# Self attention on one Trainium2 core: the values projected in tiles of 128 tokens instead of one tile per batch

## The chip, the cores and the metric

The kernel runs on one core of one Trainium2 chip. Its time is the device time of one execution in microseconds (us). Times are given for three runs of the kernel, and one further execution was recorded by the hardware profiler. A core has a matrix engine (PE, whose weight loads are listed apart as PEld), a vector engine (DVE), an activation engine (ACT), a general engine (POOL) and a sync engine (SP) that issues most of the DMAs. Each takes its instructions in order. Matrix results land in PSUM, which is divided into banks; everything else that is on the chip lies in SBUF, in 128 partitions.

## The reference

The kernel computes one decoder layer in float32 with three blocks, each followed by a residual sum and a normalisation: causal self attention (16 heads of 32), cross attention to a context of 361 tokens (16 heads of 128, four key and value heads), and a mixture of 8 experts of which each token uses 2. There are 16 batches of 100 tokens, with 512 features. The part that matters here:

```python
def _L0_attn_ref(x, w_q, w_k, w_v, w_o):            # x: 16 x 100 x 512
    q = (x @ w_q.T).reshape(b, s, NH, HD).transpose(0, 2, 1, 3)
    k = (x @ w_k.T).reshape(b, s, NH, HD).transpose(0, 2, 1, 3)
    v = (x @ w_v.T).reshape(b, s, NH, HD).transpose(0, 2, 1, 3)
    score = einsum('bhqd,bhkd->bhqk', q, k) * scale, masked causally
    o = einsum('bhqk,bhkd->bhqd', softmax(score), v)
    return o.transpose(0, 2, 1, 3).reshape(b, s, H) @ w_o.T

x = _layernorm(x + _L0_attn_ref(x, ...))
x = _layernorm(x + _L0_xattn_ref(x, ctx_2048, ...))
x = _layernorm(x + _L0_ffn_ref(x, ...))
```

The projection of the values, `x @ w_v.T`, does not know of batches: row t of the result depends on row t of x alone. The product of the softmax with v does: it needs the 100 value rows of one batch, from partition 0 on.

## The kernel before

Products in float32 precision are made from three faster ones. `split` (lines 137 to 140) writes a rounded high part of a tile on one engine and the remainder as a low part on another. `mm3` (lines 145 to 147) multiplies high by high, high by low and low by high, and `mmk` does that for the four blocks of 128 features (`KC`). So one projected tile takes 12 matmuls.

**Self attention** takes the batches in four groups (`NG`) of four (`GB`), 400 tokens each (`GT`). The input x comes transposed, features on the partitions, so x of a group is 128 x 4 x 400. A group has four chunks of 128 features, that is of four heads, and the pair of group and chunk is a unit (g, c); there are 16 units, numbered u = 4g + c. In a unit:

- `self_q` and `self_k` project 128 features of all 400 tokens, 12 matmuls each with 400 columns.
- `self_scores` makes 16 small matmuls of scores, and `self_softmax` spreads the softmax of each head j over DVE (mask and minimum, L358 and L361; sums, L367), POOL (L363 and L380) and ACT (L366 and L370).
- `self_turn` transposes the probabilities of head j on PE (L393), and ACT copies them to SBUF (L395).
- `self_attend` multiplies with the values (L405), and ACT copies the result (L415), which SP stores to DRAM as `o1d` (L416).
- `self_v(g, r)` projects the values of batch r of group g for all 512 features: 12 matmuls with the x of the batch's 100 tokens as the stationary operand and 512 columns of weights streaming. Its result has 100 rows. ACT copies it to the tile `V[g, r]` (L309). All four tiles of a group must be there when `self_attend(g, 0)` begins. PSUM results of `self_v` use the tag "mm", for group 0 the tag "t"; each tag has two banks.

The order of work inside a unit comes from a table `extra`, filled by `at(u, j, f, ...)`: f runs in unit u just before head j is turned. While unit u is turned and attended, the scores of unit u + 1 are already made, the projections of unit u + 2 are placed at j = 0 and 2, the next group's x is loaded in the unit c = 0 and split in c = 0 and 1, and its values are projected in c = 2 and 3, two tiles in each. Group 0's values are projected at the start. A scheduler then sorts the instructions by a modelled timeline, so what is written next to each other may be interleaved with other work.

**The way into the next block.** During the last units the outputs of self attention are loaded back by tiles of 128 tokens (`b_fetch`, lines 435 and 438), split (`b_split`), multiplied with w_o (`b_out`, 12 matmuls `pa`, then the residual sum and the norm on DVE), and turned (`b_xT`, L460). `b_open` closes the pool `a_x` of the inputs x, whose memory the loaded tiles `ol` and `xr` reuse. All of these have hand-set places in the units, with i = 4u + j as the position. After unit 15 the queries of the cross attention (`b_q`) follow.

Pools rotate a fixed number of buffers under one tag. The tag "f" of the pool `xp`, with two buffers, serves some of the weight chunks of 128 x 512 that are loaded and split in the first units (`chunk`), and tag "v" has eight buffers, two groups' worth.

Of the kernel before, what the change touches and what calls it, by code (L numbers as in the profile page):

```python
# [9 lines left out]
FP = mybir.dt.float32  # L10
# [7 lines left out]
B, S, D = 16, 100, 512  # L18
T = B * S
KC = D // 128  # L20
# [8 lines left out]
GB = 4  # L29
NG = B // GB  # L30
GT = GB * S
# [31 lines left out]
def tile_decoder_layer(  # L63
# [28 lines left out]
    nc = tc.nc  # L92
# [3 lines left out]
    def pool(stack, name, bufs=1, **k):  # L96
        return stack.enter_context(
            tc.tile_pool(name=name, bufs=bufs, reuse_waits="tile", **k)
        )
# [6 lines left out]
    def bank(tag, shape, name):  # L106
        return ps[-1].tile(shape, FP, name=name, tag=tag)
# [12 lines left out]
    def in_turn(ins, prev):  # L120

        if prev is not None:
            tc.add_manual_dep(
                ins.ins,
                prev.ins.name,
                mybir.DependencyInfo(
                    mybir.DependencyClass.NoSync, mybir.DependencyReason.DATA
                ),
                reason="in_turn",
            )  # L130
        return ins

    def split(dst, src, high=None, low=None):

        high, low = high or nc.scalar, low or nc.vector
        if high is nc.scalar:
            ins = nc.scalar.copy(dst.h, src)  # L137
        else:
            ins = high.tensor_copy(dst.h, src)  # L139
        low.tensor_tensor(dst.l, src, dst.h.bitcast(FP), ALU.subtract)  # L140
        return ins

    def mm3(out, a, b, start, stop):

        nc.tensor.matmul(out, a.h, b.h, start=start, stop=False)  # L145
        nc.tensor.matmul(out, a.h, b.l, start=False, stop=False)  # L146
        nc.tensor.matmul(out, a.l, b.h, start=False, stop=stop)  # L147

    def mmk(out, a, b, n=KC):
        for k in range(n):  # L150
            mm3(out, a(k), b(k), k == 0, k == n - 1)
# [44 lines left out]
    def slot_of(s):  # L196
        return Pair(WH[:, s], WL[:, s])
# [8 lines left out]
    units = {}  # L206
# [15 lines left out]
    a_l, a_r = ExitStack(), ExitStack()  # L222
    xp = pool(a_r, "a_x", 1, side="right")
    w1 = pool(a_l, "a_1", 1)
    w2 = pool(a_l, "a_2", 2)
    w3 = pool(a_l, "a_3", 8)
    ps.append(pool(a_l, "ps_a", 2, space=PSUM))
    ps_s = pool(a_l, "ps_s", 1, space=PSUM)

    xg, V, Q, K, O, P = {}, {}, {}, {}, {}, {}  # L230
# [26 lines left out]
    def chunk(n, c, queue=None):  # L257

        cc = slice(c * 128, (c + 1) * 128)
        chunks.append(n)  # L260
        p, bufs = (xp, 2) if len(chunks) % 5 > 2 else (stage, 3)
        f = p.tile([128, KC, 128], FP, name=f"f_{n}_{c}", tag="f", bufs=bufs)
        if n == "v":
            f = f.rearrange("p k n -> p (k n)")
            part, dst = src[n][:, c], units["wv_s"][:, c]
        else:
            part, dst = src[n][:, :, cc], units[f"w{n}_s"][:, :, cc]
        (queue or nc.sync).dma_start(f, part)
        return dst, f
# [24 lines left out]
    for k in range(KC):  # L294
        split(*chunk("v", k, nc.scalar), low=nc.vector if k == 2 else nc.gpsimd)

    def split_chunk(c):
        split(*chunk("q", c), nc.scalar, nc.gpsimd)
        split(*chunk("k", c), nc.scalar, nc.gpsimd)

    def self_v(g, r):
        pv = bank("mm" if g else "t", [S, D], f"pv_{g}_{r}")
        mmk(
            pv,
            lambda k: xg[g][:, k, r * S : (r + 1) * S],
            lambda k: units["wv_s"][:, k, :],
        )
        V[g, r] = w1.tile([S, D], FP, name=f"v_{g}_{r}", tag="v", bufs=8)
        nc.scalar.copy(V[g, r], pv)  # L309

    def self_q(g, c):
        cc = slice(c * 128, (c + 1) * 128)
        pq = bank("mm", [128, GT], f"pq_{g}_{c}")
        mmk(pq, lambda k: units["wq_s"][:, k, cc], lambda k: xg[g][:, k, :])

        Q[g, c] = w2.tile([128, GT], FP, name=f"qT_{g}_{c}", tag="qT")
        nc.scalar.activation(Q[g, c], pq, AF.Copy, scale=-1.0 / math.sqrt(HD1))
# [79 lines left out]
    def self_attend(g, c):  # L397

        av = bank("t", [128, GB, S], f"av_{g}_{c}")
        prev = None  # L400

        for r in range(GB):
            for j in (3, 0, 1, 2):
                h = c * 128 + 32 * j
                ins = nc.tensor.matmul(  # L405
                    av[32 * j : 32 * j + 32, r, :],
                    V[g, r][:, h : h + 32],
                    PT[g, c, j][:, r, :],
                    start=True,
                    stop=True,  # L410
                    tile_position=(0, 32 * j),
                )
                prev = in_turn(ins, prev)
        o = w2.tile([128, GT], FP, name=f"o_{g}_{c}", tag="o")
        nc.scalar.copy(o, av.rearrange("p r s -> p (r s)"))  # L415
        nc.sync.dma_start(o1d[g][:, c], o)  # L416
# [51 lines left out]
    def at(u, j, f, *a):  # L468
        extra.setdefault((u, j), []).append(lambda: f(*a))
# [24 lines left out]
    for u, (g, c) in enumerate(heads4):  # L494
        if u + 2 < NU:
            if u < 2:
                at(u, 0, split_chunk, u + 2)
            at(u, 0, self_k, *heads4[u + 2])
            at(u, 2, self_q, *heads4[u + 2])
        if g + 1 < NG:  # L500
            if c == 0:
                at(u, 1, fetch_x, g + 1)
                for k in range(2):
                    at(u, 3, split_x, g + 1, k)
            if c == 1:
                for k in range(2):
                    at(u, 1, split_x, g + 1, 2 + k)
            if c > 1:
                for r in range(2):
                    at(u, 1 + 2 * r, self_v, g + 1, 2 * (c - 2) + r)  # L510

    rows = [("wo_s", 3, kp(woT), k) for k in range(KC)]
    rows += [("wq_0", 4, Wqg[0], k) for k in range(KC)]
# [8 lines left out]
    for k in range(KC):  # L522
        i = 4 * NU - 8 + k
# [2 lines left out]
        at(i // 4, i % 4, behind, split_row, "wq_3", k)  # L526

    AHEAD = 5
    at(10, 0, b_open)
    for t, i in enumerate((44, 48, 52, 54, 58)):  # L530
        at(i // 4, i % 4, b_fetch, t)
        i += 2 if t == AHEAD - 1 else 4
        at(i // 4, i % 4, behind, b_split, t)
    for t, i in enumerate((51, 55, 59, 61, 62)):
        at(i // 4, i % 4, b_out, t)
    for t, i in enumerate((57, 60, 63)):
        at(i // 4, i % 4, b_xT, t)
# [2 lines left out]
    self_k(0, 0)  # L540
    self_scores(*heads4[0])
    self_v(0, 0)
    split_chunk(1)
    for r in range(1, GB):
        self_v(0, r)
    self_q(0, 1)
    self_k(0, 1)
    for u, unit in enumerate(heads4):
        if u + 1 < NU:
            self_scores(*heads4[u + 1])  # L550
        for j in range(4):
            for f in extra.get((u, j), []):
                f()
            self_turn(*unit, j)
        self_attend(*unit)
# [8 lines left out]
    w1 = pool(b_l, "b_1", 1)  # L564
# [113 lines left out]
    w1 = pool(c_l, "c_1", 1, side="right")  # L678
# [183 lines left out]
    for i, (b, g) in enumerate(order):  # L862
# [34 lines left out]
        if i % 3 == 2 and 8 <= i < 8 + 3 * NKV * KC:  # L897
            w, k = divmod((i - 8) // 3, KC)
# [12 lines left out]
    w1 = pool(d_l, "d_1", 1, side="right")  # L911
# [408 lines left out]
    for i in range(HEAD * NKV, len(parts)):  # L1320
        t, g = parts[i]
# [453 lines left out]
```

## Time and profile before

| | |
|---|---|
| median of 3 runs | 1432.21 us (1428.25 to 1441.84) |
| the profiled execution | 1437.28 us, its span 1435.6 us |
| mean granted clock of PE | 0.973 |
| self attention | about 0 to 207 us |
| cross-attention queries, keys and values, attention, output | about 207 to 1100 us |
| experts and the last norm | about 1100 to 1436 us |
| PE MATMUL pv of L145, L146 and L147 (self attention) | 64 each, median 392 to 394 ns |
| ACT COPY v<-pv of L309 | 16, median 585 ns |

The span runs from the first to the last instruction of the program; 1.7 us of the profiled execution's time lie outside it. Busy times are unions of the instructions' times on an engine. Matmuls overlap one another in the pipeline, so the time that one takes from a full engine is the distance between starts, not its own duration. In the views below, "L145" is line 145 of the kernel, and `pv<-WH` means that the instruction writes tile pv and reads tile WH.

### The profile page before, as it was taken

How to read it: one execution, taken by the hardware profiler on the slowest of the kernel's cores; microseconds unless marked ns; L12 is line 12 of the kernel's file. 1: busy time of each engine (PE TensorE's matmuls, PEld its weight loads, DVE VectorE, ACT ScalarE, POOL GpSimd, SP SyncE). 2: the span in 40 equal slices, each digit the busy share in tenths (PEclk: the TensorE clock that was granted, in tenths of full speed). 3: DMA queues.
4: the chain of work that ended last, by engine and by line, in shares of the span. 5: the costliest groups of instructions: out<-in, count | busy, mean ns of one | idle time of the engine just before them, and what ended most of it. 6: DMA issues, size and time to landing. Idle time of an engine off the chain costs nothing. (4 is left out here: it accounts for less than half of the span.)

```text
span 1435.6 us, 25188 instructions
## 1 busy us (share of the span) xinstructions
PE 1342.1 (93%) x7952; PEld 1107.7 (77%) x7952; DVE 954.1 (66%) x2978; ACT 746.8 (52%) x1872; POOL 731.1 (51%) x854
## 2 busy tenths in 40 slices
PE   8999989999999999999999999999999897988884
PEld 6888878888778888888888888878887674666663
DVE  5766667775567777777777667767555559653698
ACT  4666643444436666566666566656553232332353
POOL 6877653443335555555555455545444445343542
PEclk9999999999999999999999999999999998899898
DMA  5221254555442232323233222223536554666674
GB/s 157 71 92 53 70 161 111 135 92 110 98 103 62 62 74 51 74 63 75 69 75 70 74 68 69 50 65 76 131 81 200 179 165 129 210 227 214 209 239 139
DMA packets 197873, 159.79 MB, mean 111 GB/s; under 512 B 133322, under 2 KB 152878, under 8 KB 197742
## 3 DMA queue, kind: packets, MB, share of 16 engines
q1 hardware_dynamic: 187904, 137.83, 36.2%
q0 software_dynamic: 4576, 14.95, 3.4%
q10 hardware_dynamic: 5262, 5.41, 1.3%
q8 instruction: 65, 1.06, 0.3%
q14 instruction: 66, 0.54, 0.1%
HBM read 107.16 MB, written 50.99 MB: 110 GB/s over the span
## 5 line engine op out<-in xcount | busy, mean ns | idle before, releaser
L759 POOL TENSOR_SCALAR p<-p,sums 100x361 f32<-100x361 f32 x256 | 146.4, 576 | 100.3 <-DVE sums L758 89.3
L746 DVE CUSTOM_DVE_ANT_0 p<-s,nmask 100x361 f32<-100x361 f32 x256 | 132.9, 527 | 64.7 <-PE s L147 56.2
L757 ACT ACTIVATE p<-p,nm 100x361 f32<-100x361 f32 x256 | 153.2, 602 | 39.8 <-DVE nm L746 36.5
L140 DVE TENSOR_TENSOR pT_l<-ptp,pT_h 128x400 fp32r<-128x400 f32 (+1 forms) x192 | 107.4, 567 | 59.3 <-ACT pT_h L137 58.8
L145 PE MATMUL pq<-WH 128*128 128x512 f32 (+2 forms) x272 | 106.5, 392 | 6.2 <-DVE WH L139 5.8
L767 PE MATMUL ptp<-ident,p 100*128 100x100 f32 (+1 forms) x768 | 107.6, 252 | 0.0
L140 POOL TENSOR_TENSOR cT_l<-cf,cT_h 128x512 fp32r<-128x512 f32 (+1 forms) x48 | 54.4, 1134 | 104.2 <-ACT cT_h L137 102.3
L137 ACT CAST pT_h<-ptp 128x400 fp32r<-128x400 f32 (+1 forms) x192 | 91.3, 487 | 30.2 <-PE ptp L767 29.7
L767 PEld LDWEIGHTS ptp<-ident,p 100*128 100x128 f32 (+1 forms) x768 | 95.6, 152 | 13.5 <-POOL p L759 2.3
L146 PE MATMUL pq<-WL,WH 128*128 128x512 f32 (+2 forms) x272 | 104.1, 383 | 0.0
L147 PE MATMUL pq<-WH,WL 128*128 128x512 f32 (+2 forms) x272 | 103.8, 382 | 0.0
L147 PE MATMUL acc<-WH,ot_l 128*128 128x512 f32 (+1 forms) x208 | 87.3, 421 | 8.7 <-DVE ot_l L140 6.9
L145 PE MATMUL acc<-WH,ot_h 128*128 128x512 f32 (+1 forms) x208 | 87.2, 419 | 5.5 <-ACT ot_h L137 5.5
L145 PE MATMUL s<-kT_h,WH 128*100 128x362 f32 x256 | 88.5, 356 | 2.4 <-ACT kT_h L137 2.4
L145 PE MATMUL av<-pT_h,WH 128*128 128x400 f32 (+1 forms) x192 | 77.1, 401 | 11.6 <-ACT pT_h L137 11.1
L146 PE MATMUL acc<-WL,ot_h 128*128 128x512 f32 (+1 forms) x208 | 85.1, 409 | 0.0
L147 PE MATMUL s<-kT_h,WL 128*100 128x362 f32 x256 | 84.5, 330 | 0.0
L146 PE MATMUL s<-kT_l,WH 128*100 128x362 f32 x256 | 83.9, 328 | 0.0
L614 POOL TENSOR_TENSOR qs<-qs,r_q 128x512 f32<-128x512 f32 (+1 forms) x52 | 54.0, 1068 | 58.0 <-DVE r_q L169 47.5
L140 POOL TENSOR_TENSOR WL<-qf,WH 128x400 fp32r<-128x400 f32 x64 | 67.3, 1051 | 31.0 <-ACT WH L137 27.7
L145 PE MATMUL pv<-WH,cT_h 128*128 128x512 f32 (+1 forms) x192 | 80.0, 417 | 1.3 <-DVE WL L140 1.3
L145 PE MATMUL pk<-WH,cT_h 128*128 128x512 f32 (+1 forms) x192 | 77.7, 405 | 0.2
(330 smaller groups left out, 4030.0 us busy)
## 6 DMA issues: line engine op xcount, KB each, us to landing
qf<-qd SPq DMA_DIRECT2D x64, 200.0 KB
of<-od SPq DMA_DIRECT2D x48, 256.0 KB
cf<-in_ctxT SPq DMA_DIRECT2D x16, 722.0 KB
eb<-in_expert_b SPq DMA_DIRECT2D x32, 256.0 KB
ysd<-xs SPq DMA_DIRECT2D x32, 256.0 KB
f_e<-in_expert_w SPq DMA_DIRECT2D x30, 256.0 KB
f_wq<-in_Wq SPq DMA_DIRECT2D x16, 256.0 KB
f_wo<-in_Wo SPq DMA_DIRECT2D x16, 256.0 KB
```

Of the source, the lines that this page charges most:

```text
L137: ins = nc.scalar.copy(dst.h, src)
L140: low.tensor_tensor(dst.l, src, dst.h.bitcast(FP), ALU.subtract)
L145: nc.tensor.matmul(out, a.h, b.h, start=start, stop=False)
L146: nc.tensor.matmul(out, a.h, b.l, start=False, stop=False)
L147: nc.tensor.matmul(out, a.l, b.h, start=False, stop=stop)
L614: nc.gpsimd.tensor_tensor(qr[:, hs, :], qr[:, hs, :], rs[:n, hs].unsqueeze(2).to_broadcast([n, GR, HD2]), ALU.mult,)
L746: nc.vector.tensor_tensor_reduce(out=p, in0=sc[:, :SE], in1=nmask, scale=1.0, scalar=BIG, op0=ALU.add, op1=ALU.min, accum_out=nm,)
L757: nc.scalar.activation(p, p, AF.Exp, bias=nm, scale=-1.0, accum_out=sh)
L759: nc.gpsimd.tensor_scalar(p, p, sh, 1.0, ALU.mult, ALU.mult)
L767: nc.tensor.transpose(pt[:n, h, :], probs[h][:, c0 : c0 + n], ident[:S, :S])
```

## The change

A group's 400 tokens make three tiles of 128 and a rest of 16 tokens. The rests of the four groups, 64 tokens, are gathered into one more tile. So the values take 4 x 3 + 1 = 13 tiles of 12 matmuls.

- At the start, four DMAs from ACT's queue load the last 16 tokens of each group's x into `xl_f`, which DVE and POOL split into a part of weight slot 5. `self_v_last` projects these 64 tokens once and keeps them in `v_last`.
- `self_v(g, t)` now projects 128 tokens. Tile 0 is copied by ACT to `V[g, 0]`, which has 128 rows; tiles 1 and 2 are copied to `vt`, with the buffers of tag "f" in `xp`. DMAs from SP, from SBUF to SBUF, then put the rows at their batches: 28 rows of tile 0 to batch 1; 72 and 56 rows of tile 1 to batches 1 and 2; 44 and 84 rows of tile 2 to batches 2 and 3; 16 rows of `v_last` to batch 3. That is six DMAs a group.
- `self_attend` reads the first 100 rows of each V.
- Values of the next group: two tiles in the unit c = 2, one in c = 3. At the start, `self_v_last` stands between tile 0 and tiles 1 and 2.
- Since `xp` is needed longer, `b_open` moves from unit 10 to unit 12, and the first places of `b_fetch`, `b_split` and `b_out` move later.

```diff
+    w4 = pool(a_l, "a_4", 1)
...
+    REST_V = GT % 128
+    xl_f = xp.tile([128, KC, 4 * REST_V], FP, name="xl_f", tag="f", bufs=2)
+    for g in range(NG):
+        nc.scalar.dma_start(
+            xl_f[:, :, g * REST_V : (g + 1) * REST_V], xT[g][:, :, GT - REST_V :]
+        )
+    xl = slot_of(5)[:, :, : 4 * REST_V]
+    split(xl, xl_f, nc.vector, nc.gpsimd)
+    v_last = w4.tile([4 * REST_V, D], FP, name="v_last")
...
-    def self_v(g, r):
-        pv = bank("mm" if g else "t", [S, D], f"pv_{g}_{r}")
+    def self_v_last():
+        pv = bank("mm", [4 * REST_V, D], "pv_last")
+        mmk(pv, lambda k: xl[:, k, :], lambda k: units["wv_s"][:, k, :])
+        nc.scalar.copy(v_last, pv)
+
+    def self_v(g, t):
+        pv = bank("mm" if g else "t", [128, D], f"pv_{g}_{t}")
         mmk(
             pv,
-            lambda k: xg[g][:, k, r * S : (r + 1) * S],
+            lambda k: xg[g][:, k, t * 128 : (t + 1) * 128],
             lambda k: units["wv_s"][:, k, :],
         )
-        V[g, r] = w1.tile([S, D], FP, name=f"v_{g}_{r}", tag="v", bufs=8)
-        nc.scalar.copy(V[g, r], pv)
+        for r in range(GB) if t == 0 else ():
+            V[g, r] = w1.tile([128, D], FP, name=f"v_{g}_{r}", tag="v", bufs=8)
+        vt = V[g, 0] if t == 0 else xp.tile([128, D], FP, name=f"vt_{g}_{t}", tag="f", bufs=2)
+        nc.scalar.copy(vt, pv)
+        a = S if t == 0 else t * 128
+        while a < (t + 1) * 128:
+            r, o = divmod(a, S)
+            m = min(S - o, (t + 1) * 128 - a)
+            nc.sync.dma_start(V[g, r][o : o + m], vt[a - t * 128 : a - t * 128 + m])
+            a += m
+        if t == 2:
+            nc.sync.dma_start(
+                V[g, GB - 1][S - REST_V : S], v_last[g * REST_V : (g + 1) * REST_V]
+            )
...
-                    V[g, r][:, h : h + 32],
+                    V[g, r][:S, h : h + 32],
...
-            if c > 1:
-                for r in range(2):
-                    at(u, 1 + 2 * r, self_v, g + 1, 2 * (c - 2) + r)
+            if c == 2:
+                at(u, 1, self_v, g + 1, 0)
+                at(u, 3, self_v, g + 1, 1)
+            if c == 3:
+                at(u, 1, self_v, g + 1, 2)
...
-    at(10, 0, b_open)
-    for t, i in enumerate((44, 48, 52, 54, 58)):
+    at(12, 0, b_open)
+    for t, i in enumerate((48, 50, 52, 54, 58)):
         at(i // 4, i % 4, b_fetch, t)
-        i += 2 if t == AHEAD - 1 else 4
+        i += 2 if t in (0, AHEAD - 1) else 4
         at(i // 4, i % 4, behind, b_split, t)
-    for t, i in enumerate((51, 55, 59, 61, 62)):
+    for t, i in enumerate((53, 56, 59, 61, 62)):
         at(i // 4, i % 4, b_out, t)
...
-    for r in range(1, GB):
-        self_v(0, r)
+    self_v_last()
+    for t in range(1, 3):
+        self_v(0, t)
```

## The prediction

> **What bounds the kernel now.** I read the page first: its busy table, then its slices.
>
> ```profile
> span 1435.6 us, 25188 instructions
> PE 1342.1 (93%) x7952; PEld 1107.7 (77%) x7952; DVE 954.1 (66%) x2978; ACT 746.8 (52%) x1872; POOL 731.1 (51%) x854
> PE   8999989999999999999999999999999897988884
> PEclk9999999999999999999999999999999998899898
> ```
>
> The matrix engine is busy 93% of the span and full in nearly every slice, so a matmul removed from a full stretch should shorten the run by its pace. The change lives in self attention, the first 207 us, so next come busy times by stretch (columns: length, then busy us of PE, PEld, DVE, ACT, POOL, then granted clock, DMA share, GB/s).
>
> ```profile
> 45.00:90.00 45.00, 44.85 (x473) 37.68 (x472) 29.55 (x71) 28.02 (x85) 32.52 (x37) 1.00 0.24 78
> 90.00:135.00 45.00, 44.84 (x471) 37.69 (x469) 28.46 (x65) 28.56 (x83) 35.41 (x40) 1.00 0.25 85
> 135.00:165.00 30.00, 30.00 (x325) 24.18 (x324) 17.91 (x44) 19.85 (x58) 22.65 (x25) 1.00 0.16 50
> 165.00:207.00 42.00, 37.76 (x368) 31.48 (x367) 33.08 (x78) 25.09 (x68) 30.95 (x32) 0.92 0.41 121
> ```
>
> From 45 to 165 PE never rests; the others have a quarter to a third of their time free. The last 42 us, which I call the tail, are different: PE loses 4.2 us and the clock falls. The waits of PE, first in 20 to 180 us, then in 180 to 215:
>
> ```profile
> PE pv L145 <- ACT v L309: 1.3, 2, 1.1
> PE pt L393 <- POOL p L380: 0.2, 1, 0.2
> ...
> PE pt L393 <- ACT pT L395: 2.8, 2, 2.4
> PE av L405 <- ACT pT L395: 1.4, 2, 0.8
> ```
>
> Last the timeline of PE. It gives the pace of a value matmul (start to start, which a busy time of 0.39 us hides, since matmuls overlap), and the tail's gap with the slow stretch after it:
>
> ```profile
> 151.94 0.45 PE L145 MATMUL pv<-WH 128*100 128x512 f32 x1
> ...
> 154.54 0.39 PE L147 MATMUL pv<-WH,WL 128*100 128x512 f32 x1
> 154.77 0.51 PE L393 MATMUL pt<-ident,p 100*100 100x100 f32 x4
> ...
> 191.13 0.55 PE L393 MATMUL pt<-ident,p 100*100 100x100 f32 x4 [2.38 <-ACT pT L395]
> ...
> 196.76 0.63 PE L145 MATMUL pa<-WH,olp_h 128*128 128x512 f32 x1
> 197.19 0.63 PE L146 MATMUL pa<-WL,olp_h 128*128 128x512 f32 x1
> ...
> 199.05 0.40 PE L145 MATMUL pa<-WH,olp_h 128*128 128x512 f32 x1
> 199.29 0.40 PE L146 MATMUL pa<-WL,olp_h 128*128 128x512 f32 x1
> ```
>
> One value tile of 12 matmuls takes 154.77 - 151.94 = 2.83 us of PE. After the gap of 2.38 us a matmul takes 0.43 us until 198.8, then 0.24 again.
>
> **What the Trainium skill says.** "TensorE: Matmul & The Clock Gate", Step-by-step: a matmul costs what it streams, one moving column a cycle; how many output rows it has does not enter. The trace agrees: pv with 100 rows runs at 0.231 us, pa with 128 rows at 0.228. So a 128-token tile costs PE what a 100-token tile costs. Same page, Part 1: the clock halves when PE has been idle in a window of some 3.4 us. Here a shorter gap, 2.38 us, was followed by nearly half the pace, so the measurement decides. "DMA: Bandwidth & Descriptors", Anatomy of one DMA: about 2.0 us fixed plus bytes over 436 GB/s. The trace has no copy inside SBUF; its nearest kind is the 200 KB store of o, whose landing mark comes 1.9 us after issue when alone and up to 5 us among bulk loads. The same page, "Why a DMA increments its semaphore by 16 and not by 1": the engines used are the largest number up to 16 that divides the rows, so 44 rows use 11 and 28, 56 and 84 use 14: no copy falls on a single engine. No run here shows that yet.
>
> **The change, part by part.**
>
> *Matmuls removed.* 16 tiles become 13: 36 of 192 value matmuls go (PE's built program shrinks from 7200 to 7164 rows). The first group still runs four tiles (0, 1, 2 and the shared rest of 64 rows), so the start gains nothing; each later group loses one tile, in its predecessor's last unit. 3 x 2.83 = 8.5 us, all where PE is full.
>
> *Weight loads.* 128 columns instead of 100: 188 ns for 164 (the rows of pa and pv). Both are under the pace of 231, so hidden; uncovered they would be 156 x 24 ns = 3.7 us.
>
> *Evictions.* ACT makes 13 copies instead of 16 at 585 ns: 1.8 us less, of no worth on an engine with a third free.
>
> *V copies.* 24 new DMAs on SP, six a group. About 0.33 us of issue each, 8 us of an SP that mostly waits (83 us for o alone). 2.5 MB more traffic: 1200 packets of 2 KB at 84 ns over 16 engines, 6 us of a queue busy 20%. Latency I bound between 1.9 us (lone store) and 5.5 (among loads) and take 2.2. Who waits: the first attend matmul of a group, and behind it PE's whole queue. From the end of tile 2 to that attend PE has two projections (2.2 us each), two score blocks (0.9 each), an attend and four or more transposes: about 10 us. The path is eviction 0.6, two issues 0.7, landing 2.2, with ACT's queue ahead perhaps 1 to 2: some 5.5. Hidden with 4 us to spare; at 5.5 us of latency just hidden. Cost 0, at most 1 us a group.
>
> *The shared rest at the start.* Four loads on ACT's queue, 2048 packets of 64 B at 11 ns (as the 64 B packets of ol took): 1.4 us on each DMA engine. ACT issues them while it waited anyway (0.53 and 0.91 us idle before f_q and qT), and the f_q cast moves behind qT. The cast of 128x256 is half of 0.43 us on DVE and the low part half of 1.3 us on POOL, between 16 and 22 us, where DVE had 3.0 us idle. The load of f_q for chunk 2 now waits for a slot of vt, so for two V copies: it moves from 11.8 us to about 24.5, lands near 27.5, and its cast stands in ACT's queue ahead of the first big exponentials (27.3 before). POOL's low part then ends near 30.5; PE asks for it at 34.15. Against that, two matmuls of the rest fill part of the 1.1 us wait for a PSUM bank. Bounds -0.5 and +1.5; I take 0.
>
> *The tail.* b_open moves from unit 10 to 12, since the pool of x now lives until the last vt is copied; the loads of ol and xr move past the V copies on SP, the splits of ol and two of the five output projections (12 matmuls pa each) later. In the built order 36 pa matmuls followed the last scores; now 46 to 48 do, and DVE takes the last softmax before the norm of tile 0. The PE work from the first transpose of unit 12 to the last attend is equal: pq and pk 3 x 2.2, five pa blocks 5 x 2.76, scores 1.8, attends 3.4, transposes about 7.5, sum some 33 to 35 us. Before, it ran from 165.2 to 206.9, 41.7 us: 4.2 us of waits and about 2.8 us from the slow clock. Walking the new order with the durations of before, the last scores end near 15 us after that first transpose, their softmax near 25 (POOL, with two ol splits ahead of it, is the latest), and PE asks for it at 30. The transposes of unit 14 then wait on ACT and DVE for 1 to 2 us in pieces instead of 2.4 in one, so the slow clock should not come. Bounds 0 and 7; I take 5.
>
> *Later stages.* The order is the same up to the experts; there some loads, stores and transposes move by a few places. PE has 63 us idle in the last 436, so it can go either way; I take 0, bounds -4 and +4.
>
> *Sum.* 1437.3 (the profiled execution's own time; 1.7 of it lies outside the span) - 8.5 - 5 = 1423.8. The median of the runs is 5.1 below that execution, so 1432.2 - 13.5 = 1418.7, say 1419.
>
> **Rivals.**
>
> (B) Only the matmuls count: the tail is bound by the chain score, softmax, ACT copy, which starts 8.5 us sooner but stalls as before. For: it was ACT, not PE, that ended the tail's waits. Against: more pa work now covers it. 1432 - 8.5 = 1424.
>
> (C) The gain is lost: softmax of the short units falls behind once the long unit has 2.83 us less cover. For: the first transposes of units 1 and 6 had under 1.5 us between POOL's end and their start. Against: those units hold as many matmuls before as after; where a tile goes, the spare was 7 us or more. 1429 to 1433.
>
> (D) Slower: V copies land late. Place: the first attend of each group, PE's queue behind it. Price: if eviction to landing takes 13 us and not 5.5, a wait of 3 us, and after it the clock as in the tail, 2.5 us more: 4 x 5.5 = 22, less 8.5: 1446. It decides from about 10 us, and costs more than the gain from 12. For: SP is in order, and a V copy stands behind stores that waited up to 21 us for ACT. Against: the stores ahead of it belong to earlier units, done by then.
>
> (E) More: the whole tail, 7 us, and 4 in the experts: 1432 - 8.5 - 11 = 1413.
>
> That the change doesn't do what it says is excluded by the count of matmuls.
>
> **How the numbers follow.** Forecast 0.48 (own range 1413 to 1424), B 0.16, C 0.08, D 0.08, E 0.20. One per cent, about what a measurement of this kernel can tell from no change, is 14.3 us: a line at 1417.9, just under the forecast. Half of the forecast's cases lie beyond it, so faster is 0.24 + 0.20 and a little of B, 0.45; same 0.24 + 0.15 + 0.08 = 0.47; slower 0.08. The range of 1407 to 1434 takes in E with its bound, B and C, and leaves out D.
>
> **What would show it.** Right: 156 value matmuls; PE waits of under 1 us up to 160 us; the first matmul of the cross-attention queries (206.8 before) at 192 to 196; no stretch at 0.43 us a matmul in the tail; all later stages as long as before. B: that matmul at 198 with a gap of over 2 us on ACT. C: waits of transposes for POOL. D: PE waits at av for a DMA into v. Wrong altogether: later stages longer or shorter by over 5 us.

## The result, and the profile after

The changed kernel takes 1440.52 us (median of 20 runs, 1432.43 to 1446.62); the kernel before takes 1433.59 us in the 20 runs taken with it. The ratio is 1.004, with a 95% interval of 1.0026 to 1.0055. So it is slower by four tenths of a per cent, where I had forecast 1419 us and a range of 1407 to 1434.

The profiled execution of the changed kernel took 1443.94 us. First its page (busy time of the engines, then PE and its granted clock in 40 slices):

```profile
span 1442.2 us, 25189 instructions
PE 1342.3 (93%) x7916; PEld 1111.0 (77%) x7916; DVE 956.9 (66%) x2979; ACT 745.0 (52%) x1869; POOL 734.3 (51%) x855
PE   6999979999999999999999999999999996988885
PEclk9999999999999999999999999999999898899997
```

PE has 36 instructions fewer (7916 for 7952), as the change says, and the same busy time to 0.2 us. Up to the end of self attention PE is busy 4.7 us less; the later stages, whose order hardly changes, add 4.9 us. So the busy sum of the whole tells nothing here. The slices show where to look: the first holds 6 tenths instead of 8, and the sixth, from 180 to 216 us, 7 instead of 8.

I cut self attention at three marks that the timeline of PE gives: the start of the first `av` (attend), the end of the last `s<-kT,qT` (scores), the end of the last `av`. What I call the tail from here on begins at the last scores; the tail of the prediction was longer and began at 165 us.

| stretch, us | before | changed | difference |
|---|---|---|---|
| start to the first attend | 40.1 | 46.7 | +6.6 |
| first attend to last scores | 144.6 | 136.1 | -8.5 |
| last scores to last attend (the tail) | 22.2 | 30.1 | +7.8 |
| last attend to the end | 1228.7 | 1229.4 | +0.7 |

The sum is the 6.6 us between the two spans. The middle seems to pay what the removed matmuls promised. The start and the tail take it back nearly twice. The first query matmul of the cross attention, forecast at 192 to 196 us, starts at 212.8.

Busy times by stretch (columns: length, then busy us of PE, PEld, DVE, ACT, POOL, then granted clock, DMA share, GB/s), first one line of before for a stretch that I have not shown yet, then the changed kernel:

```profile
20.00:45.00 25.00, 24.68 (x220) 22.04 (x221) 16.29 (x39) 13.02 (x40) 19.09 (x22) 1.00 0.13 43
...
20.00:45.00 25.00, 20.18 (x126) 17.89 (x126) 10.33 (x24) 8.62 (x28) 14.99 (x17) 0.86 0.26 79
45.00:90.00 45.00, 43.09 (x482) 37.05 (x482) 31.21 (x72) 27.20 (x82) 32.36 (x38) 1.00 0.27 81
90.00:135.00 45.00, 43.72 (x482) 38.24 (x475) 33.51 (x73) 28.26 (x81) 37.18 (x41) 1.00 0.21 69
135.00:165.00 30.00, 30.00 (x316) 25.73 (x315) 18.77 (x45) 20.14 (x58) 24.50 (x28) 1.00 0.28 89
165.00:207.00 42.00, 35.70 (x378) 28.22 (x377) 34.25 (x82) 24.32 (x72) 28.72 (x30) 1.00 0.47 142
```

From 20 to 45 us PE is busy 20.2 us (24.7 before) at a clock of 0.86 (1.00 before). From 45 to 135 it loses 3.2 us where it lost 0.3, and DVE is busier in the same time (64.7 us for 58.0). In the last stretch it loses 6.3 us for 4.2. That stretch ends at 207 us and shows the full clock; in the next 6 us, which still belong to the tail of the changed kernel, the granted clock is 0.60. The waits of PE up to 215 us name the releasers:

```profile
PE pt L424 <- ACT pT L426: 6.0, 4, 2.4
...
PE pk L145 <- ACT v_last L317: 4.8, 1, 4.8
PE pa L147 <- POOL olp_l L140: 1.6, 1, 1.6
```

The second line is new, at the start. The first and the third lie in the tail, but for 1.3 us of the first.

**The start.** The timeline of the changed kernel from 23 to 33 us, all engines, cut to what matters:

```profile
23.13 1.65 SPq L335 DMA_DIRECT2D v<-vt  x2
...
27.12 0.38 SPq L269 DMA_DIRECT2D f_q<-in_wqT  x1
...
30.00 0.62 ACT L137 CAST WH<-f_q 128x512 fp32r<-128x512 f32 x1 [4.97 <-DMA f_q<-in_wqT]
30.52 0.96 ACT L397 ACTIVATE p<-p 100x400 f32<-100x400 f32 x2
...
31.39 0.56 ACT L317 COPY v_last<-pv_last 64x512 f32<-64x512 f32 x1
...
32.00 0.70 PE L145 MATMUL pk<-WH 128*128 128x400 f32 x1 [4.82 <-ACT v_last L317]
...
32.50 0.54 PE L146 MATMUL pk<-WL,WH 128*128 128x400 f32 x1
...
32.83 0.54 PE L147 MATMUL pk<-WH,WL 128*128 128x400 f32 x1
```

Read it as a chain. Two V copies out of the first `vt` are issued from 23.13 us and have landed at 26.98. Only then is its buffer free for the load of `f_q`, issued at 27.12. ACT, in order, sits 4.97 us in front of the cast of that load. Behind the cast stand exponentials and then the eviction of `v_last`, and `pk` needs the PSUM bank that `pv_last` holds until then. PE waits 4.82 us. After that gap its matmuls start 0.33 us apart instead of 0.18, up to 37 us.

**The tail.** DVE from 183 us:

```profile
183.14 1.05 DVE L389 TENSOR_TENSOR p<-s,causal 100x400 f32<-100x400 f32 x2
184.11 2.42 DVE L161 SCALAR_TENSOR_TENSOR t_ln<-y_ln,v_ln 128x1 f32<-128x1 f32 x1
186.45 0.56 DVE L389 TENSOR_TENSOR p<-s,causal 100x400 f32<-100x400 f32 x1
```

and POOL at the same time:

```profile
184.00 2.51 POOL L140 TENSOR_TENSOR olp_l<-ol,olp_h 128x512 fp32r<-128x512 f32 x2
```

A norm instruction on 128 single numbers, which takes 0.22 us elsewhere in the same trace, takes 2.42 us. It ends when POOL's two splits end. Half of the last unit's softmax (L389) waits behind it. PE has two long waits in the tail, 2.40 us at 195 us and 2.33 us at 208 us, both for ACT's copy of a transpose. What ACT did before each of the two copies, with PE's first wait and the issues of SP:

```profile
193.86 0.20 ACT L157 ACTIVATE a_ln<-v_ln 128x1 f32<-128x1 f32 x1 [1.66 <-DVE v_ln L179]
...
194.67 0.49 ACT L426 COPY pT<-pt 100x400 f32<-100x400 f32 x1
...
195.22 0.55 PE L424 MATMUL pt<-ident,p 100*100 100x100 f32 x4 [2.40 <-ACT pT L426]
...
201.79 0.33 SPq L484 DMA_DIRECT2D x1d<-xr  x1
202.17 1.24 SPq L466 DMA_DIRECT2D ol<-o1d  x2
...
206.88 0.62 ACT L137 CAST olp_h<-ol 128x512 fp32r<-128x512 f32 x1 [2.26 <-DMA ol<-o1d]
```

The first copy is of unit 14, not of the late softmax of unit 15. It stands behind an activation of the second norm, for which ACT waited 1.66 us on DVE, and DVE worked on that norm between the sums of the late softmax. The second copy, at 207.40 us, stands behind a cast that waited 2.26 us for the load of `ol`. The load was issued right behind the store `x1d`, which waits for a finished norm. From 208.9 us on, after the second wait, PE's transposes start 0.17 to 0.27 us apart instead of 0.09 to 0.13: the clock of 0.60.

### The profile page after: what moved, and what is told of

Read it like the earlier page. It is cut to its first block, busy times and chain, and to the rows that moved or that the text cites. A ratio compares the mean times of both kernels' runs of the same rounds, so it can differ in the third digit from the quotient of the medians.

```text
span 1442.2 us, 25189 instructions
## 1 busy us (share of the span) xinstructions
PE 1342.3 (93%) x7916; PEld 1111.0 (77%) x7916; DVE 956.9 (66%) x2979; ACT 745.0 (52%) x1869; POOL 734.3 (51%) x855
## 4 chain that ended last, share of the span: by engine, by line
PE 55%; DVE 17%; DMA 13%; ACT 5%; issue 5%; SPq 2%; POOL 1%; another core or an unknown queue 0%; ACTq 0%; DVEq 0%; POOLq 0%
DMA f_wo<-in_Wo 4%; PE ptp L801 3%; PE pk L145 3%; PE pv L145 3%; PE pv L147 3%; PE pv L146 3%; PE pk L146 3%; PE pk L147 3%; PE acc L147 2%; PE s L145 2%; PE acc L145 2%; PE s L147 2%; PE s L146 2%; PE pq L145 2%; PE acc L146 2%
```

## The experiments

All marks are read as above, from one trace each; a ratio is that of the runs to runs of the kernel before on the same chip. Those runs had medians from 1428.1 to 1431.5 us. A second trace of the kernel before tells how far a mark can be trusted:

> The kernel before, unchanged, for a second trace beside the experiments: in self attention the same times as in the first trace within 0.5 us (first attend 40.1, last scores 184.7, last attend 206.9); what differs after 400 us is not of the change.

First attend 39.7, last scores 184.2, last attend 206.5: 0.4 us from the first trace. But the rest took 1217.5 us instead of 1228.7, 6.3 of the difference between 396 and 998 us. So I compare traces up to the last attend only, and whole times by ratios.

| kernel | first attend | last scores | last attend | tail | ratio to before (95%) |
|---|---|---|---|---|---|
| before, two traces | 40.1, 39.7 | 184.7, 184.2 | 206.9, 206.5 | 22.2, 22.3 | 1 |
| changed | 46.7 | 182.8 | 212.8 | 30.1 | 1.004 (1.0026 to 1.0055) |
| own | 39.2 | 179.4 | 205.4 | 25.9 | 0.9992 (0.9977 to 1.0008) |
| own_2x | 38.9 | 179.2 | 205.1 | 25.9 | 0.9982 (0.9958 to 1.0007) |
| own_oldtail | 39.3 | 178.9 | 205.8 | 26.9 | 0.9989 (0.9973 to 1.0005) |
| tail_only | 39.8 | 181.9 | 208.7 | 26.9 | 1.001 (0.9991 to 1.0029) |
| fewer | 39.4 | 178.4 | 203.5 | 25.1 | 0.9988 (0.9975 to 1.0001) |
| even | 38.8 | 172.5 | 205.9 | 33.3 | 1.0003 (0.9986 to 1.0019) |
| even_xt | 38.6 | 172.3 | 202.5 | 30.2 | 0.9964 (0.9952 to 0.9977) |
| even_dve | 39.0 | 172.8 | 200.0 | 27.2 | 0.9948 (0.9916 to 0.998) |
| even_xt_dve | 39.2 | 172.9 | 201.2 | 28.3 | 0.9945 (0.9926 to 0.9965) |
| before_xt_dve | 39.3 | 184.1 | 206.9 | 22.9 | 0.9995 (0.9978 to 1.0013) |
| after_dve | 47.2 | 184.2 | 211.3 | 27.1 | 1.0048 (1.003 to 1.0066) |

### own: the start alone

```diff
-    xl_f = xp.tile([128, KC, 4 * REST_V], FP, name="xl_f", tag="f", bufs=2)
+    xl_f = xp.tile([128, KC, 4 * REST_V], FP, name="xl_f", tag="xl", bufs=1)
...
-        vt = V[g, 0] if t == 0 else xp.tile([128, D], FP, name=f"vt_{g}_{t}", tag="f", bufs=2)
+        vt = V[g, 0] if t == 0 else xp.tile([128, D], FP, name=f"vt_{g}_{t}", tag="vt", bufs=2)
```

> The changed kernel, but vt and xl_f with buffers of their own in the pool xp, so that the load of the q weights of chunk 2 no longer waits for a vt buffer. Theory A (the start is lost because that load is late: its cast on ACT ended a chain exponentials, eviction of v_last, PE at pk): the first attend matmul returns from 46.7 us to 40 to 42, the PE gap of 4.8 us at 32 us goes, the tail stays as in the changed kernel (30 us from the last scores to the last attend), in all some 6 us less than the changed kernel, about 1434. Rival (the shared rest itself, its loads, casts and matmuls, or the V copies delay the start): the first attend stays above 44 us and the time at 1438 or more.

The first attend is at 39.2 us and the last at 205.4, both 7.5 us sooner than in the changed kernel, and the time is level with before (1428.49 us beside 1429.3). The busy times show the stretch whole again:

```profile
20.00:45.00 25.00, 25.00 (x226) 22.64 (x225) 17.60 (x43) 14.16 (x46) 20.17 (x23) 1.00 0.21 68
```

All the loads of weight chunks now stand before the V copies in SP's queue, and `v_last` is evicted at 22.04 us, before the exponentials. Theory A holds for the start: the rest tile's own loads, casts and matmuls are still there and cost nothing that shows at the first attend. Two things I had not expected. The tail did not stay at 30 us, as I wrote; it is 25.9 us. Part of that is the mark: an attend and three pa matmuls lie ahead of the last scores again. From the first transpose of unit 12 to the last attend own takes 44.5 us and the changed kernel 44.9, with five query matmuls (0.9 us) fewer in it; before took 41.7 with those of own. So only some 1.3 us at the end go back to the late start. And in the middle the last scores come only 5 us sooner than in before, though 36 pv matmuls are gone from it and 9 of pa moved behind it, 10.4 us at their pace. ACT and PE around 99 us, ACT first:

```profile
98.49 0.54 ACT L397 ACTIVATE p<-p 100x400 f32<-100x400 f32 x1 [1.25 <-POOL p L394]
98.93 0.57 ACT L330 COPY v<-pv 128x512 f32<-128x512 f32 x1
```

```profile
99.55 0.50 PE L145 MATMUL pv<-WH 128*128 128x512 f32 x1 [1.65 <-ACT v L330]
...
100.97 0.63 PE L147 MATMUL pv<-WH,WL 128*128 128x512 f32 x1
101.40 0.63 PE L145 MATMUL pv<-WH 128*128 128x512 f32 x1
```

The eviction of a value tile waits in ACT's order behind an exponential that waits for POOL, and PE waits for the bank. After that gap of 1.65 us matmuls start 0.43 us apart for 3 us.

### own_2x: are the V copies on the path?

The `dma_start` of each V copy stands twice.

> As own (vt and xl_f with their own buffers), with every V copy issued twice, so 48 copies inside SBUF instead of 24. If V copies cost nothing on the path: first attend, last scores and last attend within 0.5 us of own (39.2, 179.4, 205.4), time within 2 us of own. Rival (the copies, in SP's queue ahead of other loads and in front of attend, are part of what was lost): the last attend 2 us or more later.

All three marks are within 0.3 us of own. With buffers of their own, V copies cost nothing on the path. In the changed kernel the 24 of them took 1.96 to 4.35 us from issue to landing, median 2.8.

### own_oldtail and tail_only: the places of the tail

own_oldtail is own with `vt` of the last group in the pool `stage`, which lets the tail have its old places; tail_only is the kernel before with the new places:

```diff
-    at(10, 0, b_open)
-    for t, i in enumerate((44, 48, 52, 54, 58)):
+    at(12, 0, b_open)
+    for t, i in enumerate((48, 50, 52, 54, 58)):
...
-        i += 2 if t == AHEAD - 1 else 4
+        i += 2 if t in (0, AHEAD - 1) else 4
...
-    for t, i in enumerate((51, 55, 59, 61, 62)):
+    for t, i in enumerate((53, 56, 59, 61, 62)):
```

> The kernel before with nothing but the new places of b_open, b_fetch, b_split and b_out (16 value tiles as before, no V copies). Theory A: last scores to last attend 28 to 30 us instead of 22, of which 2.8 us are pa matmuls that before came earlier; the total is some 5 us longer, about 1438. Rival (V copies in SP's queue did it): the tail's total length from 165 us to the last attend unchanged, time 1433.

> As own, and vt of the last group in the pool stage, so that b_open, b_fetch, b_split and b_out stand at the places of the kernel before. Theory A (the tail is lost because these were put later): last scores to last attend back from 30 us to 22 to 24, two blocks of pa again before the last scores, total about 1425 to 1428. Rival (the tail is lost because V copies stand in SP's queue and because it starts sooner than its loads): still 28 us or more, total about 1433.

tail_only's last attend is 1.8 to 2.2 us later than before. Nine pa matmuls crossed the last scores (2.1 us), and PE idles 2.5 us more in the tail; the new waits are for DVE's norms and splits (1.8 and 0.8 us). So the new places cost about 2 us at the last attend, less than I expected, and the whole time can't be told from no change. But putting the old places back in own_oldtail did not bring the tail back: 26.9 us, not 22 to 24, though 24 pa matmuls (two blocks) lie before the last scores again, and its last attend, 205.8 us, is no sooner than that of own. With 13 tiles the places are not what keeps the tail long.

### fewer: the matmuls alone

```diff
-                for r in range(2):
+                for r in range(2 if c == 2 else 1):
...
         nc.scalar.copy(V[g, r], pv)
+        if g and r == 2:
+            V[g, 3] = V[g, 2]
```

> The kernel before without the fourth value tile of groups 1 to 3: the third tile is used for batch 3 too (left out: the values of three batches; everything else is done). 36 matmuls less and no copies, no shared rest, no new places. If matmuls on a full PE are worth their pace: 8.5 us less, about 1425, the last scores at 176. Rival (the softmax of the next unit loses its cover): transposes wait for POOL and half or less is gained, 1429 or more.

This kernel leaves out the values of three batches, so that nothing but matmuls is gone. The rival comes out. Of 8.5 us of matmuls 3.0 to 3.4 us are left at the last attend; the ratio is 0.9988. Three of the 8.5 go in the middle: it is 5.6 us shorter, and PE idles 2.5 us there (0.3 before). Three more go in the tail, which grows from 22.2 to 25.1 us. The busy times of the last stretch, then the two longest waits of PE in the stretch from 38 to 207 us:

```profile
165.00:207.00 42.00, 34.85 (x337) 28.60 (x336) 30.43 (x80) 23.23 (x65) 28.56 (x30) 0.85 0.46 136
```

```profile
PE pt L395 <- ACT pT L397: 4.5, 3, 4.0
PE av L407 <- ACT pT L397: 3.6, 3, 2.7
```

PE is busy 34.9 of 42 us (37.8 before) at a clock of 0.85 (0.92 before). The waits name ACT, where my rival named POOL; but the longest, 4.0 us, is for a copy behind exponentials for which ACT had itself waited 1.5 and 1.1 us on POOL. What bounds the tail isn't PE, so PE's earlier arrival turns into waiting.

### even: one value tile a unit

```diff
-            if c == 2:
-                at(u, 1, self_v, g + 1, 0)
-                at(u, 3, self_v, g + 1, 1)
-            if c == 3:
-                at(u, 1, self_v, g + 1, 2)
+            if c > 0:
+                at(u, 4 - c, self_v, g + 1, c - 1)
```

> As own, but with one value tile in each of the units c = 1, 2, 3 instead of two in c = 2 and one in c = 3. Theory S (in the units that lose a tile, PE is no longer the longest engine: POOL and ACT with the softmax, splits and evictions are, so waits and the slow clock after them eat the matmuls' gain): with the tiles spread, the waits of PE between the first attend and the last scores fall from 3.3 us to 1 to 1.5, the slow stretch after 99.6 us goes, last scores at 176 to 177 instead of 179.4, in all 2 to 3 us less than own. Rival P (the waits come from the tail's and the loads' order, not from how PE's work is spread): the last scores stay at 179 or later.

Theory S holds for the middle, by more than I wrote: PE idles 0.1 us between the first attend and the last scores, and those come at 172.5 us, 6.9 before own; some 1.3 us of that are an attend and two pa matmuls that moved behind them. And the time is that of before. All of it is lost in the tail, now 33.3 us long. The two stretches:

```profile
90.00:135.00 45.00, 45.00 (x469) 38.88 (x468) 29.91 (x73) 28.77 (x87) 37.73 (x43) 1.00 0.22 69
...
165.00:207.00 42.00, 31.50 (x277) 24.84 (x266) 32.57 (x70) 21.08 (x60) 25.45 (x26) 0.87 0.45 130
```

The timeline, all engines, shows who does it:

```profile
183.27 1.67 POOL L411 TENSOR_TENSOR p<-p,rinv 100x400 f32<-100x400 f32 x2 [0.34 <-DVE rinv L410]
183.69 4.94 DVE L161 SCALAR_TENSOR_TENSOR t_ln<-y_ln,v_ln 128x1 f32<-128x1 f32 x1
...
184.90 1.28 POOL L140 TENSOR_TENSOR olp_l<-ol,olp_h 128x512 fp32r<-128x512 f32 x1
...
186.14 1.26 POOL L140 TENSOR_TENSOR WL<-f_wq,WH 128x512 fp32r<-128x512 f32 x1
187.36 1.26 POOL L140 TENSOR_TENSOR olp_l<-ol,olp_h 128x512 fp32r<-128x512 f32 x1
...
190.12 0.33 SPq L484 DMA_DIRECT2D x1d<-xr  x1
190.14 0.22 DVE L161 SCALAR_TENSOR_TENSOR t_ln<-y_ln,v_ln 128x1 f32<-128x1 f32 x1
...
190.24 1.09 PE L491 MATMUL ptx<-ident,xr 128*128 128x128 f32 x4 [3.95 <-DVE xr L181]
```

Five POOL instructions run without a break from 183.27 to 188.62. The norm instruction of DVE begins at 183.69 and ends at 188.63. The same instruction takes 0.22 us at 190.14, when POOL is idle. This matches "SBUF — State Buffer" of the Trainium skill, Who interferes with whom: DVE, when it reads two operands from SBUF, and GpSimd (here POOL) share one pair of ports, which is locked for a whole instruction, and the other engine blocks. `y_ln` and `v_ln` both lie in SBUF. Read so, the lock passed four times from one POOL instruction to the next before DVE had it. The other traces agree: in all of them together this instruction takes over 0.5 us 38 times in the first 220 us, and each time it ends within 0.07 us after the end of a POOL instruction. Behind the norm the transposes of the normed tile hold PE for 3.95 us. The store `x1d` of that tile, issued at 190.12, holds SP's queue, in which nothing had been issued since 180.79: the loads of `ol` behind it land from 197.0 us on, and ACT waits 5.2 us for the first.

### even_xt: the transposes later

```diff
-    for t, i in enumerate((57, 60, 63)):
+    for t, i in enumerate((60, 62, 63)):
```

> As even, and the transposes of the normed tiles (b_xT) put later, at 60, 62, 63 instead of 57, 60, 63, so that they don't hold a PSUM bank of the softmax transposes while DVE is behind. If that bank made the 2.7 us wait in the tail: the wait falls under 1.5 us, the slow clock after it too, last scores to last attend 22 to 24 us instead of 26, another 2 to 3 us less. Rival (the wait is for the softmax of the last units itself, whatever is beside it): still 25 us or more.

The last attend comes 3.4 us sooner than in even and the ratio is 0.9964. The tail is 30.2 us, though, not 22 to 24, so the bank was not the main cause. What differs in the trace is that PE no longer stands in front of a late norm: it does pa blocks meanwhile. A norm instruction of 0.16 us is still held, now for 2.65 us.

### even_dve, even_xt_dve, before_xt_dve, after_dve: less POOL work beside the norms

```diff
-        return split(OL[t][:, :, :n], ol[:, :, :n], low=nc.gpsimd)
+        return split(OL[t][:, :, :n], ol[:, :, :n], low=nc.vector)
```

> As even, with the low part of the loaded output tiles (olp_l) made on DVE instead of POOL. Theory L (in the tail a norm instruction of DVE that takes 0.2 us alone is held for as long as POOL works without a break, 4.94 us at 183.7 us in even; behind it the last norm, the store x1d and with it SP's queue of loads are late): without olp_l in POOL's queue POOL's run behind the norm is 3 us shorter, the 4.94 us fall to under 2.5, the PE gap of 3.95 us falls to under 1.5, last scores to last attend from 33.3 to 28 or less, 4 to 5 us in all. Rival Q (the loads in SP's order or the PSUM banks hold the tail): the DVE row gets longer by 5 x 0.7 us and the tail stays at 32 us or more.

Theory L holds. The tail falls from 33.3 to 27.2 us, although DVE has five splits more to do, and the ratio to before is 0.9948. PE's wait for the normed tile falls from 3.95 to 0.2 us, though one of 4.3 us for ACT comes up before an attend. The two splits of `ol` are gone from POOL's run, and the norm instruction is held 2.9 us less:

```profile
184.34 2.06 DVE L161 SCALAR_TENSOR_TENSOR t_ln<-y_ln,v_ln 128x1 f32<-128x1 f32 x1
```

> As even_xt, with olp_l on DVE too. Theory L: the held norm instructions (2.65 us at 184.8 and 1.48 us at 187.5 in even_xt) fall under 1 us, last scores to last attend from 30.2 to 27 or 28, time 1420 to 1421 beside 1428 of before. Rival Q: no change against even_xt, 1423 to 1424.

The last attend is at 201.2 us and the ratio 0.9945: not to be told from even_dve or even_xt by their intervals. The two long ones of even_xt went, but later norm instructions are still held (an L161 for 1.2 us, an L181 for 1.5), and in this order PE waits 4.5 us for the last normed tile. Like even_xt and even_dve it is faster than before, here by half a per cent: 1423.93 us beside 1431.52.

> The kernel before (16 value tiles, no V copies) with the tail of even_xt_dve: new places, b_xT at 60, 62, 63, olp_l on DVE. What the 36 matmuls are worth with the same tail: if the tail no longer takes them back, this is 6 to 8 us longer than even_xt_dve, about 1427; if the tail's own chain sets the end whatever comes before, the two are within 3 us.

This is the nearest measure of the 36 matmuls. With the old 16 tiles the same places of the tail give 206.9 us at the last attend and a ratio of 0.9995; with 13 tiles spread evenly, 201.2 us and 0.9945. The change with its spread is worth 5.7 us at the last attend and 0.5% in all, once the start and the tail let it through. How much of that is the spread is open: no run spreads 16 tiles anew. The new tail alone is worth nothing that can be measured.

> The changed kernel as it is, with nothing but olp_l made on DVE instead of POOL. Start and middle stay as in the changed kernel (first attend 46.7, last scores 182.8). Theory L: the norm instruction held for 2.42 us at 184.1 us, in front of the last softmax, is no longer held, and last scores to last attend falls from 30.1 to 27 us or less; the time 3 us under the changed kernel, about level with before. Rival Q: the tail stays at 29 us or more because the late start and the loads set it.

The tail shrank by 2.9 us to 27.1 and the norm instruction at 184 us to 0.8, as theory L says. The 3 us in all that I had forecast did not come. But the built order moved elsewhere too, the last scores came 1.4 us later, and the last attend only 1.5 us sooner. The ratio did not move (1.0048 beside 1.004). With the start lost, this repair alone does not show in the time.

## Why the prediction was wrong

Two of its terms failed most: the start, put at 0, cost 6.6 us, and the tail, put at a gain of 5, lost. The third, the removed matmuls, was put at 8.5 us and gave about half of that. Its steps, one by one:

- *Matmuls removed*: 156 value matmuls, as counted, and their pace is theirs. But the step put all of them "where PE is full" and took that as gained. The middle's -8.5 only looks like it: 12 pa matmuls and an attend moved out of it into the tail (some 3.6 us together), and 2.9 us more of PE's idle time came in. A cut at the first transpose of unit 12 is cleaner, since all removed matmuls lie ahead of it and all pa blocks behind. From the first attend to there the time falls from 125.1 to 121.3 us, so 3.8 us were gained; 2.9 of the rest are idle time, 0.9 are five query matmuls that moved ahead of the cut, and 0.9 I can't place. The step forgot that a unit which loses a tile also loses the cover of its neighbours. My check in rival C, a spare of 7 us or more where a tile goes, looked at each transpose by itself, not at the evictions in ACT's order. fewer has 2.5 us and own 4.0 us of idle time there, even 0.1.
- *Weight loads and evictions*: of no worth, as said; the middle of even runs at full pace with both.
- *V copies*: cost 0, right (own_2x), apart from the buffer that they hold (the next step). The latency I took, 2.2 us, was short of the median of 2.8; the fit with 2.0 us that I quoted from "DMA: Bandwidth & Descriptors" of the Trainium skill, Anatomy of one DMA, is made on DMAs that GpSimd (POOL) issues, and these are issued by SP. The engines that I counted from the rows agree with the trace: copies of 44 rows raise their semaphore in 12 steps and those of 28, 56 and 84 rows in 15, one step more than the 11 and 14 engines. SP spends 0.6 to 1.0 us on the issue of each, not 0.33 (the two shown above take 1.65).
- *The shared rest at the start*: taken as 0 with a bound of 1.5; it was 6.6. This is the error whose cause is shown best. I had found the very load and its cause, and put its landing at 27.5 us; it was 29.98, since the two copies that free its buffer had landed only at 26.98. The sequel is what I left out. I followed the cast to the exponentials and to POOL's low part, which PE needs at 34 us. I did not ask what else stood behind the cast on ACT. The eviction of `v_last` did, and it held the bank of `pk`, which PE wanted at 27.2 us. The slow pace then nearly doubled the price of the next dozen matmuls. own, which changes nothing but two buffer tags, takes away 7.5 us.
- *The tail*: a gain of 5 with a bound of 0; it lost. By the measure of that step, from the first transpose of unit 12 to the last attend, 41.7 us became 44.9, though five query matmuls had moved out of it, so the error is 8.2 us, the largest of all. (From the last scores on it is 7.8 us more: some 3.6 for what moved in, 3.8 for PE's idle time.) fewer, with the old places and no copies, takes 44.6 us by the same measure, so the missing matmuls alone can bring most of the loss: a tail that waits for other engines does not get shorter with work taken from PE ahead of it. The walk had the last scores right, 15 us after that transpose, but forecast waits of 1 to 2 us in place of 8.0. I had walked the new order with the durations of before. DVE's norm instructions have no fixed duration: 0.2 us, or up to 2.42 us here while POOL works on, and the new places put two splits of `ol` on POOL just where a norm fell, ahead of the last softmax. The trace of before had it already: one L161 takes 1.73 us at 195.3, and the next ones 0.2 to 1.3.
- *Later stages*: 0 within 1 us, as said. The traces of one and the same kernel differ there by more.

Of the rivals, C came nearest. It priced the lost cover at 5 to 9 us (1429 to 1433 beside B's 1424), and fewer loses 5.1 to 5.5 of its 8.5 us; but C looked for PE's waits at POOL, and they are at ACT. D had a wait at the start, but saw it at `av` for a V copy that lands late, and not at the load that a V copy holds up. None had the tail's lock.

What stays open: which of the waits at the end of the changed kernel come from the new places, and which from the missing matmuls. After the first transpose of unit 12 the same matmuls take some 4.1 us more (3.2, and 0.9 for the five that moved out). Of these own takes off 1.3 with the start; tail_only shows 2.1 with the places alone and fewer 2.9 with the missing matmuls alone. They overlap, and no run parts them. That POOL holds DVE's norms is shown for the tail of even; for the whole time of the changed kernel after_dve shows no gain from freeing them.

## What to carry to other kernels

A gap in front of a chain is not gained by removing work ahead of it: before pricing a saving, ask which engine ends the stage, and follow the saving to the last wait of that stage. When a new tile takes a buffer from a rotating tag, list what is allocated next in that tag, and then all that stands behind *that* on its in-order queue, to the last PSUM bank. If an instruction's durations in one trace spread from 0.2 to 1.7 us, look for what it shares with another engine before using their median.

## What the hardware showed that I had not expected

- A DVE instruction on 128 single numbers was held for 4.94 us by five POOL instructions in a row, and for 2.42 us by two. It waited out every one, and took 0.2 us when POOL was idle.
- The slow pace of PE after a gap does not follow from the gap's length. A gap of 1.65 us in own was followed by 3 us at 0.43 us a matmul, and one of 2.40 us at 195 us in the changed kernel by none: its later pa matmuls started 0.23 us apart. One of 2.33 us at 208 us in the same trace was followed by slow matmuls up to 215 us. "TensorE: Matmul & The Clock Gate" of the Trainium skill, Part 1, says that the clock falls after an idle window of some 3.4 us, and that the window runs freely. All three gaps are shorter than that. No run here shows what decides.
